# Values evicted by ScalarE, the first experts' products moved behind the routing, and a weight place opened sooner, in a two-layer graph network

## The chip, the core and the metric

The kernel runs on one core of a Trainium2 chip. A time is the device time of one execution in microseconds; the kernel before is given by the median of 4 runs. The engines are called as in the profile: PE is TensorE, DVE is VectorE, ACT is ScalarE, POOL is GpSimd, and SP is the queue that issues most of the DMAs. Each engine executes its own instructions in the order in which they are written, and waits in that order.

## The reference

384 nodes with 1024 features each, fp32, pass two layers. What matters here:

```python
xn = _layernorm(x)
x = x + _L0_gnn_ref(xn, edges, types, ...) + _L0_mix_ref(xn, ...)
x = x + _L0_ffn_ref(_layernorm(x), ...)
xn = _layernorm(x)
x = x + _L1_gnn_ref(xn, ...) + _L1_mix_ref(xn, ...)
x = x + _L1_ffn_ref(_layernorm(x), ...)

# L0_gnn: attention over the graph's edges, 16 heads
q = x @ wq.T + bq; k = x @ wk.T + bk; v = x @ wv.T + bv
q2 = q @ wiq.T + biq; k2 = k @ wik.T + bik; v2 = v @ wiv.T + biv
mask = -inf; mask[src, dst] = softplus(type_weight)[edge_type - 1]   # the last edge of a cell counts
attn = softmax(q2 @ k2.T / 8 + mask); out = attn @ v2
return out @ wo.T + bo

# L0_mix: q = softplus(q / scale), k likewise; linear attention, here over sequences of one node
# L0_ffn: logits of 8 experts from x @ wqkv.T (a small attention of 8 by 8 for each node), top 2 of 8,
#         y = (silu(a) * g) @ w2[e].T with a, g = split(x @ w1[e].T), weighted by softmax of the two
# L1_ffn: one of 8 experts by the nearest centroid of x,
#         y = x + relu((xhat * gamma[e] + beta[e]) @ w1[e] + b1[e]) @ w2[e] + b2[e], mixed with x by a sigmoid
```

A row of `attn` sums to 1, so a bias on `v2` comes out of the attention as the same bias on `out`.

## The kernel before, in words

Nodes lie in three blocks of 128 (`nb`), features in eight pieces of 128 (`KC`), and halves of 512 (`hf`). A projection is written either with its result transposed, features on the partitions (`proj_t`, the matmul at L136, `w` fixed and 384 nodes as the moving side), or with nodes on the partitions (`proj_n`, L148, 512 features as the moving side). A scheduler writes each engine's order from the program's order and its estimates, so a line of the code that is moved can land in another place on each engine.

The stages, with their time in the profiled execution:

- 0 to 15 us: the norm of the input, and its transposes into `xnT` (L203, L217, L218).
- 15.6 to 222 us: the projections q, k, then q2, k2 and v. Meanwhile POOL builds the edge mask: the edges' keys are written out and read back in every order (`keys`), DVE compares them to find repeated cells, and POOL writes 96 columns of types into a table of cells in memory, one indirect DMA after the other (`lastd`, L469); each waits for an earlier one of its table. The cells are blanked before by SP's DMAs. The table is read back into `last`.
- 222 to 265 us: `v2` (L148 for `wiv`). Its six PSUM blocks are evicted by DVE with a broadcast bias row (L551). The router's column sums `sums` (L556), eight matmuls with a matrix of ones, and their copy `wsum` (L557) come last. `kind` (L568) and the following lines to L586 turn `last` into the additive `mask` on DVE.
- 277 to 469 us: a loop over eight pairs of heads. For a pair, `scores` (L614) for each block writes one PSUM place `sc` (there is one), DVE scales and masks it into `s` (L616) and takes the row maximum `rs` (L619), ACT takes exps (L621), DVE the normalisation `rr`, `pr` (L624, L627). Between them stand the blocks of the mix heads (`mix_block`, L655), whose softplus takes ACT's pieces z, az and a few more and DVE's L229 to L232, and `values` for the pair before, whose result is copied to `oT`. `inv` and `binv` (L599 to L603) are small constants of the mix heads.
- 469 to 582 us: the output projections (L703) and the first routing, block by block. `to_router(nb)` transposes x, multiplies with the router `wr` (L746) and norms the block; `to_places(nb)` does the top 2 on DVE (L354 to L378, `both` L755), and then `place_both`: `rank` on PE (L385), `own` on DVE (L388), and the gather of the first two experts' nodes by a product with `own`, `first` (L758, 8 matmuls a block that are each recorded twice). `first` collects over the three blocks and is copied to `xe` (L770, L771). POOL scatters the normed rows to `xg0` for the other experts.
- 583 to 714 us: the experts of layer 0 (L896, L923).
- 725 to 930 us: layer 1's graph part and mix heads. Its start waits for a gather `yt` of the experts' results.
- 930 to 994 us: the projection `w_fc` (L1105) and the second routing, built like the first: `mix_norm` (L1116, L1117), transposes, `x` times centroids `cen` (L1138), norms, `near` (L1160), `place` (`rank` L328, `slotf` L337), `own` (L1169), `first` (L1172), and its eviction with the experts' gamma and beta (`scaled`, L961 to L968).
- 996 to 1079 us: the experts of layer 1 (`h` L1311, `t` L1320, `y` L1335, L1337), the rows of the others read by SP (`xs`, L1300).

Weights are loaded by SP in one order into a ring of places (`ring`, `next_w`), each load waiting until its place has been read. There are three places from the start, one (`w_top`) more from the attention, two more (`w_more`) from the first routing, and one (`w_last`) that `experts1_sorted` opens.

The places differ in when they open: a pool's memory can be taken when the pools that lay there before have been closed and read.

## Time and profile before

| | |
|---|---|
| median of 4 runs | 1081.91 us (1077.88 to 1086.05) |
| the profiled execution | 1087.65 us, its span 1085.8 us |
| mean granted clock of PE | 0.973 |
| PE busy | 1022.4 us, 94% of the span |
| DVE, ACT, POOL busy | 349.0, 267.1, 317.5 us |
| memory traffic | 172 GB/s over the span; 399 GB/s in the second of 40 slices (27 to 54 us) |

A busy share is over the whole span. A row of the timeline gives start, duration, engine, line, operation, result and sources, the shapes, and in brackets the engine's idle time just before and what ended it. A row with x16 is a run of 16 records of one kind; an fp32 matmul leaves two records. `PEclk` and the durations of records of one shape tell which clock PE had: a run of 16 records of 128x128 by 128 spans about 2 us at full clock and 3.8 at half.

### The profile page before, as it was taken

How to read it: one execution, taken by the hardware profiler on the slowest of the kernel's cores; microseconds unless marked ns; L12 is line 12 of the kernel's file. 1: busy time of each engine (PE TensorE's matmuls, PEld its weight loads, DVE VectorE, ACT ScalarE, POOL GpSimd, SP SyncE). 2: the span in 40 equal slices, each digit the busy share in tenths (PEclk: the TensorE clock that was granted, in tenths of full speed). 3: DMA queues.
4: the chain of work that ended last, by engine and by line, in shares of the span. 5: the costliest groups of instructions: out<-in, count | busy, mean ns of one | idle time of the engine just before them, and what ended most of it. 6: DMA issues, size and time to landing. Idle time of an engine off the chain costs nothing. (4 is left out here: it accounts for less than half of the span.)

```text
span 1085.8 us, 9492 instructions
## 1 busy us (share of the span) xinstructions
PE 1022.4 (94%) x3453; PEld 552.4 (51%) x3453; DVE 349.0 (32%) x966; ACT 267.1 (25%) x493; POOL 317.5 (29%) x276
## 2 busy tenths in 40 slices
PE   6999999997799999999997999969999999997896
PEld 4555555543455555544555666434444466555332
DVE  4580000006676667621332111051306000554121
ACT  3111111100576666620112111221302010122211
POOL 2152355564787668600001000130002000014100
PEclk9999999999899999999997999979999999998998
DMA  9949623226223432523165988968522222136992
GB/s 340 399 157 408 161 88 146 79 80 186 11 0 41 117 78 0 156 78 126 58 199 208 318 311 289 380 230 324 193 78 78 78 78 83 72 117 245 360 410 111
DMA packets 69973, 186.53 MB, mean 172 GB/s; under 512 B 21416, under 2 KB 22280, under 8 KB 69664
## 3 DMA queue, kind: packets, MB, share of 16 engines
q1 hardware_dynamic: 41216, 150.19, 38.4%
q0 software_dynamic: 24688, 29.40, 11.1%
q10 hardware_dynamic: 4016, 6.27, 1.6%
q8 instruction: 29, 0.48, 0.2%
q14 instruction: 24, 0.20, 0.1%
HBM read 161.29 MB, written 25.06 MB: 172 GB/s over the span
## 5 line engine op out<-in xcount | busy, mean ns | idle before, releaser
L469 POOL DMA_INDIRECT countd<-seen,cells x96 | 153.2, 1596 | 62.6 <-DMA countd<-seen,cells 38.2
L136 PE MATMUL mm<-xnT,w 128*128 128x384 f32 x512 | 165.7, 486 | 0.3 <-DVE xnT L218 0.3
L655 PE MATMUL mm<-xnT,w 128*128 128x384 f32 x384 | 133.4, 495 | 0.0
L136 PEld LDWEIGHTS mm<-xnT,w 128*128 128x128 f32 x512 | 97.1, 190 | 67.9 <-DVE xnT L218 0.6
L469 POOL DMA_INDIRECT lastd<-typ,cells x96 | 96.2, 1002 | 118.7 <-DMA lastd<-typ,cells 75.2
L655 PEld LDWEIGHTS mm<-xnT,w 128*128 128x128 f32 x384 | 71.0, 191 | 57.4 <-issue 14.9
L703 PE MATMUL mm<-w,t 128*128 128x512 f32 x192 | 84.5, 594 | 0.8 <-DVE x L402 0.8
L148 PE MATMUL mm<-w,xnT 128*128 128x512 f32 x192 | 82.8, 592 | 0.0
L136 PE MATMUL mm<-t,w 128*128 128x384 f32 x256 | 82.7, 486 | 0.0
L896 PE MATMUL h<-w,xeT 128*128 128x352 f32 x224 | 68.3, 462 | 0.7 <-DVE xeT L888 0.3
L136 PEld LDWEIGHTS mm<-t,w 128*128 128x128 f32 x256 | 48.6, 190 | 33.9
L148 PEld LDWEIGHTS mm<-w,xnT 128*128 128x128 f32 x192 | 36.3, 190 | 45.5 <-issue 45.5
L568 DVE TENSOR_TENSOR kind<-last 128x1152 f32<-128x1152 f32 x1 | 1.4, 1358 | 177.1 <-DMA last<-lastd 177.1
L703 PEld LDWEIGHTS mm<-w,t 128*128 128x128 f32 x192 | 35.8, 190 | 43.6 <-issue 41.7
L896 PEld LDWEIGHTS h<-w,xeT 128*128 128x128 f32 x224 | 41.9, 190 | 24.4 <-DVE xeT L888 2.4
L1005 PE MATMUL mm<-w,xnT 128*128 128x512 f32 x96 | 43.6, 613 | 1.3 <-DVE xnT L218 1.3
L292 POOL DMA_INDIRECT xg<-xn,slot x3 | 4.0, 1323 | 139.4 <-DVE xn L1116 122.6
L1105 PE MATMUL mm<-w,oT 128*128 128x512 f32 x96 | 42.7, 595 | 0.0
L923 PE MATMUL y<-w,hT 128*128 128x512 f32 (+1 forms) x96 | 41.6, 592 | 0.0
L148 PE MATMUL mm<-w,t 128*128 128x512 f32 x96 | 41.4, 592 | 0.0
L516 ACT ACTIVATE t<-mm,cols 128x384 f32<-128x384 f32 x24 | 13.9, 580 | 107.3 <-PE mm L136 98.1
L1060 POOL TENSOR_TENSOR x<-x,gb 128x1024 f32<-128x1024 f32 x3 | 7.3, 2427 | 98.4 <-DVE x L1059 98.4
(297 smaller groups left out, 1188.3 us busy)
## 6 DMA issues: line engine op xcount, KB each, us to landing
w<-in_w1s SPq DMA_DIRECT2D x16, 1408.0 KB, 7.7
w<-in_xw SPq DMA_DIRECT2D x8, 2048.0 KB, 15.9
w<-in_xw2s SPq DMA_DIRECT2D x8, 2048.0 KB, 14.9
w<-in_w2s SPq DMA_DIRECT2D x8, 1536.0 KB, 10.8
keys<-keyd POOLq DMA_DIRECT2D x4, 1536.0 KB
xg<-blank SPq DMA_DIRECT2D x12, 512.0 KB, 11.5
w<-in_wk SPq DMA_DIRECT2D x2, 2048.0 KB
w<-in_mwq SPq DMA_DIRECT2D x2, 2048.0 KB, 7.8
```

Source lines behind the costliest of these rows:

```text
L136: mm(ps[:, :N], lhsT=w[:, j, kc, :], rhs=rhs[:, kc, :], start=kc == 0, stop=kc == KC - 1)
L148: mm(ps, lhsT=lhs[:, kc, nb * P:(nb + 1) * P], rhs=w[:, kc, :], start=i == 0 and kc == 0, stop=i == len(pairs) - 1 and kc == KC - 1)
L292: i = gp.indirect_dma_start(rows, bass.IndirectOffsetOnAxis(ap=at, axis=0), src, None, bounds_check=n - 1, oob_is_err=False)
L469: gp.indirect_dma_start(cells[:, :], bass.IndirectOffsetOnAxis(ap=at[:, i, c:c + 1], axis=0), src[:, c:c + 1], None, bounds_check=N * N + ...
L516: ac.activation(dst[:, ob, :], ps, AF.Identity, bias=cols[:, i, ob:ob + 1], scale=1.0)
L655: mm(ps[:, :N], lhsT=w[:, j, kc, :], rhs=xnT[:, kc, :], start=kc == 0, stop=kc == KC - 1)
L703: mm(pss[hf], lhsT=src[:, kc, nb * P:(nb + 1) * P], rhs=w_out[("mwo", "wo")[part]][hf][:, kc, :], start=part == 0 and kc == 0, stop=part = ...
L896: mm(ag[i][:, :F0], lhsT=xeT[kc // 4][:, kc % 4, :], rhs=w1[kc // 4][:, kc % 4, i * F0:(i + 1) * F0], start=kc == 0, stop=kc == KC - 1)
L923: mm(y, lhsT=hT[:k, e, j, :], rhs=w2[:k, e % 2 * len(K2) + j, :], start=j == 0, stop=j == len(K2) - 1)
L1005: mm(ps, lhsT=xnT[:, kc, nb * P:(nb + 1) * P], rhs=ws[hf][:, kc, :], start=kc == 0, stop=kc == KC - 1)
L1060: gp.tensor_tensor(x[:, b, :], x[:, b, :], gb[:, 1, :], OP.add)
L1105: mm(ps, lhsT=oT[:, kc, nb * P:(nb + 1) * P], rhs=ws[hf][:, kc, :], start=kc == 0, stop=kc == KC - 1)
```

## The change

- The values' six blocks are copied out of PSUM by ACT, without the bias; the bias `biv` is added later, by feature, when `oT` leaves PSUM (a tenth column of `cols`). The broadcast rows `brow` shrink from three to two.
- The router weight `wr` is loaded first on ACT's queue, and the column sums and `wsum` are made at the start. `inv` and `binv` are made behind the second block's norm.
- The small inputs of the last stage (`b1x`, `gbx`, `cen`) are loaded by SP behind `brow`, where they were loaded by ACT's queue.
- In both routings the products `first` of blocks 0 and 1 are issued behind the last block's router, and that of block 2 behind its places. `own` is kept for all blocks. The centroids' sums `csum`, which stood at the start of layer 1, stand in the first routing behind the products of blocks 0 and 1.
- In layer 1 the buffers `ed_w`, `z`, `y`, `em` and `kv` lie in a pool `mid` that is closed ahead of the `w_fc` projections; `w_last` is opened there, and is the next place in the ring.

```diff
...
+    b1x = const.tile([P, FC1], F32, name="b1x")
+    gbx = const.tile([P, 2, X, KC], F32, name="gbx")
+    cen = const.tile([P, KC, X], F32, name="cen")
+    csum = const.tile([P, X], F32, name="csum")
     rest = ExitStack()
     with ExitStack() as layer:
         act = layer.enter_context(tc.tile_pool(name="act0", bufs=1))
...
         with tc.tile_pool(name="edges", bufs=1) as ed, tc.tile_pool(name="hot", bufs=2) as hot, \
                 tc.tile_pool(name="work0", bufs=2) as work, \
                 tc.tile_pool(name="ps_a", bufs=8, space=PSUM) as pa:
+            ac.dma_start(wr, d["wqkv"])
             ids = ed.tile([P, 3, EC], I32, name="ids")
             ac.dma_start(ids, d["ids"])
...
             wq = [load_t(d["wq"][hf], apart=hf == 0) for hf in range(2)]
...
-            cols = const.tile([P, 9, KC], F32, name="cols")
+            cols = const.tile([P, 10, KC], F32, name="cols")
             ac.dma_start(cols, d["cols"])
+            ps = pa.tile([P, HB], F32, tag="mm", name="sums")
+            for kc in range(KC):
+                mm(ps[:, :3 * X], lhsT=ones_q, rhs=wr[:, kc, :], start=kc == 0, stop=kc == KC - 1)
             ready(AF.Sqrt, eps)
             for nb in range(NB):
                 mean, rinv = norm_block(x[:, nb, :])
                 xn = work.tile([P, D], F32, tag="xn", name="xn")
                 norm_on_both(xn, x[:, nb, :], mean, rinv)
                 copied = to_t(pa, xnT, xn, nb)
+            with tc.issue_after(copied[0].ins):
+                ve.tensor_copy(wsum, ps[:, :3 * X])
             alike = ed.tile([P, P], F32, name="alike")
...
             proj_t(pa, "wq", xnT, biased(qT, 0), wq)
             kT = hidden()
             proj_t(pa, "wk", xnT, biased(kT, 1))
-            brow = ed.tile([P, 3, D], F32, name="brow")
+            brow = ed.tile([P, 2, D], F32, name="brow")
             with tc.issue_after(loads[-1].ins):
-                nc.sync.dma_start(brow, bass.AP(tensor=d["brow"].tensor, offset=d["brow"].offset, ap=[[0, P], [D, 3], [1, D]]))
-                nc.sync.dma_start(wr, d["wqkv"])
+                nc.sync.dma_start(brow, bass.AP(tensor=d["brow"].tensor, offset=d["brow"].offset, ap=[[0, P], [D, 2], [1, D]]))
+                nc.sync.dma_start(b1x, d["b1"])
+                nc.sync.dma_start(gbx[:, 0], d["xgamma"])
+                nc.sync.dma_start(gbx[:, 1], d["xbeta"])
+                nc.sync.dma_start(cen, d["cen"])
             q2T = act.tile([P, KC, N], F32, tag="q2T", name="q2T")
             proj_t(pa, "wiq", qT, biased(q2T, 3))
             with tc.issue_after(loads[-1].ins):
...
             vT = hidden()
             proj_t(pa, "wv", xnT, biased(vT, 2))
             for nb in range(NB):
-                for i in (1, 2):
+                for i in range(2):
                     ve.tensor_tensor(x[:, nb, :], x[:, nb, :], brow[:, i, :], OP.add)
             v2 = act.tile([P, NB, D], F32, tag="v2", name="v2")
             def values_in(hf, nb, ps):
                 cs = slice(hf * HB, (hf + 1) * HB)
-                ve.tensor_tensor(v2[:, nb, cs], ps, brow[:, 0, cs], OP.add)
+                ac.copy(v2[:, nb, cs], ps)
             proj_n(pa, [("wiv", vT)], values_in)
-            ps = pa.tile([P, HB], F32, tag="mm", name="sums")
-            for kc in range(KC):
-                mm(ps[:, :3 * X], lhsT=ones_q, rhs=wr[:, kc, :], start=kc == 0, stop=kc == KC - 1)
-            ve.tensor_copy(wsum, ps[:, :3 * X])
...
             with tc.issue_after(copied[1].ins):
                 ac.activation(eta, etw, AF.Abs)
             softplus(etp, etw, eta, 4)
+            inv = act.tile([P, KC], F32, name="inv")
+            with tc.issue_after(copied[1].ins):
+                ac.activation(inv, cols[:, 8, :], AF.Exp, scale=-1.0)
+            ve.tensor_scalar(inv, inv, 1.0 / 8.0, None, op0=OP.mult)
+            binv = act.tile([P, 2, KC], F32, name="binv")
+            for i in range(2):
+                ve.tensor_tensor(binv[:, i, :], cols[:, 5 + i, :], inv, OP.mult)
             kind = ed.tile([P, NB, N], F32, name="kind")
             ve.tensor_tensor(kind, lasts[0], lasts[1], OP.max)
...
-            inv = at.tile([P, KC], F32, name="inv", bufs=1)
-            ac.activation(inv, cols[:, 8, :], AF.Exp, scale=-1.0)
-            ve.tensor_scalar(inv, inv, 1.0 / 8.0, None, op0=OP.mult)
-            binv = at.tile([P, 2, KC], F32, name="binv", bufs=1)
-            for i in range(2):
-                ve.tensor_tensor(binv[:, i, :], cols[:, 5 + i, :], inv, OP.mult)
...
                         h = 2 * hp + r
                         mm(ps[r * DH:(r + 1) * DH, :N], lhsT=v2[:, mb, h * DH:(h + 1) * DH], rhs=prT[r][:, mb, :],
                            start=mb == 0, stop=mb == NB - 1)
-                ve.tensor_copy(oT[:, hp, :], ps[:, :N])
+                ve.tensor_scalar(oT[:, hp, :], ps[:, :N], cols[:, 9, hp:hp + 1], None, op0=OP.add)
             w_mix = {}
...
         def row(cols, name, dtype=F32):
             return kp.tile([P, *cols], dtype, name=name)
-        keep = {"xe0": [row([KC // 2, P], f"xe0_{g}") for g in range(2)], "oh": row([NB, X], "oh4"), "most": row([NB], "most4"),
+        keep = {"xe0": [row([KC // 2, P], f"xe0_{g}") for g in range(2)], "oh": row([NB, X], "oh4"), "own": row([NB, P], "own4"), "most": row([NB], "most4"),
                 "slot": row([NB], "slot4", I32), "info": row([NB, 2], "info4"),
                 "slots": row([NB, 2], "slots6", I32), "share": row([2, NB], "share6")}
...
                 oh = route_block(*queries[nb], share[:, 1, nb:nb + 1])
                 ve.tensor_tensor(both[:, nb, :], oh[0], oh[1], OP.add)
                 place_both(px, slots[:, nb, :], own0[:, nb, :], both, oh, nb)
+                scatter(xg0[:, :], [slots[:, nb, i:i + 1] for i in range(2)], [xn[:, nb, :]] * 2, X * CAP0)
+            def to_first(nb):
                 for kc in range(KC):
                     mm(first[kc // 4][:, kc % 4, :], lhsT=xn[:, nb, kc * P:(kc + 1) * P], rhs=own0[:, nb, :],
                        start=nb == 0 and kc % 4 == 0, stop=nb == NB - 1 and kc % 4 == 3)
-                scatter(xg0[:, :], [slots[:, nb, i:i + 1] for i in range(2)], [xn[:, nb, :]] * 2, X * CAP0)
             for nb in range(1, NB):
                 pss = halves(pm)
...
                 project(nb, 1, pss)
                 to_places(nb - 1)
             to_router(NB - 1)
+            for nb in range(NB - 1):
+                to_first(nb)
+            ps = px.tile([P, HB], F32, tag="x", name="sums")
+            for kc in range(KC):
+                mm(ps[:, :X], lhsT=ones_q, rhs=cen[:, kc, :], start=kc == 0, stop=kc == KC - 1)
             to_places(NB - 1)
+            to_first(NB - 1)
             ve.tensor_copy(keep["xe0"][0], first[0])
             ac.copy(keep["xe0"][1], first[1])
...
+            ve.tensor_copy(csum, ps[:, :X])
             over0 = too_many(px, "x", both, CAP0)
...
     K2V = P + 2
-    b1x = const.tile([P, FC1], F32, name="b1x")
-    ac.dma_start(b1x, d["b1"])
-    gbx = const.tile([P, 2, X, KC], F32, name="gbx")
-    ac.dma_start(gbx[:, 0], d["xgamma"])
-    ac.dma_start(gbx[:, 1], d["xbeta"])
-    cen = const.tile([P, KC, X], F32, name="cen")
-    ac.dma_start(cen, d["cen"])
     def scaled(dst, src, g, es):
...
+            mid = ExitStack()
+            part = mid.enter_context(tc.tile_pool(name="mid", bufs=1))
             a_bc = act.tile([P, 2, D], F32, tag="rows", name="a_bc")
-            ed_w = act.tile([P, NB, N], F32, name="ed_w")
-            if keep is not None:
-                csum = act.tile([P, X], F32, name="csum")
-                ps = px.tile([P, HB], F32, tag="x", name="sums")
-                for kc in range(KC):
-                    mm(ps[:, :X], lhsT=ones_q, rhs=cen[:, kc, :], start=kc == 0, stop=kc == KC - 1)
-                ve.tensor_copy(csum, ps[:, :X])
+            ed_w = part.tile([P, NB, N], F32, name="ed_w")
             xn1 = act.tile([P, NB, D], F32, name="xn1")
             xnT = act.tile([P, KC, N], F32, tag="byf", name="xnT2")
...
                    lambda hf, nb, ps: ac.copy(vh[:, nb, hf * 4:hf * 4 + 4, :P], ps.rearrange("p (a b) -> p a b", b=P)))
             if taken:
                 held(loads[-2:], taken)
-            kv = act.tile([P, KC, K2V], F32, name="kv")
+            kv = part.tile([P, KC, K2V], F32, name="kv")
             threes = (range(0, 3), range(3, 6), range(6, 8))
             for hps in threes:
                 n = len(hps)
...
                 to_t(pm, oT, o, nb)
             ws = [load_w(d["w_fc"][hf]) for hf in range(2)]
+            mid.close()
+            if keep is not None:
+                w_last = rest.enter_context(tc.tile_pool(name="w_last", bufs=LAST, side="right", reuse_waits="tile"))
+                ring[:0] = [w_last] * LAST
             def project(nb, hf):
                 ps = pm.tile([P, HB], F32, tag="mm", name="mm")
                 for kc in range(KC):
...
             xT = act.tile([P, KC, N], F32, tag="kq", name="xT4")
             oh, most, slot = keep["oh"], keep["most"], keep["slot"]
             first = [px.tile([P, HB], F32, tag="x", name="first").rearrange("p (a b) -> p a b", b=P) for _ in range(2)]
+            own = keep["own"]
             sums, last = {}, []
             def to_router(nb):
...
                 slotf = small.tile([P, 1], F32, tag="slotf", name="slotf")
                 place(px, "x", slotf, oh, oh, nb, CAP)
-                own = work.tile([P, HB], F32, tag="y", name="own")[:, :P]
-                ve.tensor_scalar(own, rowf[:, :P], slotf, None, op0=OP.is_equal)
+                ve.tensor_scalar(own[:, nb, :], rowf[:, :P], slotf, None, op0=OP.is_equal)
                 ve.tensor_copy(slot[:, nb:nb + 1], slotf)
-                for kc in range(KC):
-                    mm(first[kc // 4][:, kc % 4, :], lhsT=xb[:, kc * P:(kc + 1) * P], rhs=own,
-                       start=nb == 0 and kc % 4 == 0, stop=nb == NB - 1 and kc % 4 == 3)
                 with tc.issue_after(scatter(xg[:, :], [slot[:, nb:nb + 1]], [xb], X * CAP).ins):
                     gp.tensor_tensor(x[:, nb, :], x[:, nb, :], fb, OP.add)
                     last[:] = [scatter(bg[:, :], [slot[:, nb:nb + 1]], [x[:, nb, :]], X * CAP)]
+            def to_first(nb):
+                for kc in range(KC):
+                    mm(first[kc // 4][:, kc % 4, :], lhsT=xn1[:, nb, kc * P:(kc + 1) * P], rhs=own[:, nb, :],
+                       start=nb == 0 and kc % 4 == 0, stop=nb == NB - 1 and kc % 4 == 3)
             for hf in range(2):
                 project(0, hf)
...
                 project(nb, 1)
                 to_places(nb - 1)
             to_router(NB - 1)
+            for nb in range(NB - 1):
+                to_first(nb)
             to_places(NB - 1)
+            to_first(NB - 1)
             for g in range(2):
                 scaled(keep["xe0"][g], first[g], g, (0, 1))
             at = [slot[:, nb:nb + 1] for nb in range(NB)]
...
     def experts1_sorted(xe0):
-        with tc.tile_pool(name="w_last", bufs=LAST) as w_last, \
-                tc.tile_pool(name="act4", bufs=1) as act, \
+        with tc.tile_pool(name="act4", bufs=1) as act, \
...
-            ring.extend([w_last] * LAST)
```

## The prediction

> **What bounds the kernel now.** I read the busy shares first, then the list of waits of TensorE (PE), then the timeline around the long waits. PE works for 1022.4 of 1085.8 us, so the change can win only inside the 63 us in which PE stands still, inside work that it takes off PE (little), or by the clock. The longest waits of PE (columns: what waited for what, total us, times, longest):
>
> ```profile
> engine line waited for: us in total, times, longest us
> PE sc L614 <- DVE wsum L557: 11.8, 1, 11.8
> PE mm L217 <- DVE xn L203: 10.3, 1, 10.3
> PE mm L217 <- DMA yt<-yg,slots: 8.7, 1, 8.7
> PE rank L385 <- DVE both L755: 5.0, 1, 5.0
> ```
>
> The first and the last lie where the change works; the second is the start (unchanged), the third the gather between the layers. The timeline at the first (start, us, engine line operation, idle before and who ended it):
>
> ```profile
> 263.34 1.86 PE L556 MATMUL sums<-wr,ones_q 128*128 128x24 f32 x16
> ...
> 273.22 3.67 DVE L551 TENSOR_TENSOR v<-mm,brow 128x512 f32<-128x512 f32 x6
> ...
> 276.81 0.17 DVE L557 COPY wsum<-sums 128x24 f32<-128x24 f32 x1
> 276.96 1.28 ACT L599 ACT_TABLE_LOAD   x1 [54.04 <-DVE v L551]
> ...
> 277.04 1.65 PE L614 MATMUL sc<-k2T,q2T 64*128 64x384 f32 x4 [11.84 <-DVE wsum L557]
> ...
> 278.87 0.95 DVE L616 SCALAR_TENSOR_TENSOR s<-sc,mask 128x768 f32<-128x768 f32 x1
> ```
>
> The reader sees that PE has all of its operands by 265.2, and that DVE, in its own order, evicts the six value blocks only after the mask chain (254.26 to 273.22), which starts when `last` has been read back:
>
> ```profile
> L568 DVE TENSOR_TENSOR kind<-last 128x1152 f32<-128x1152 f32 x1 | 1.4, 1358 | 177.1 <-DMA last<-lastd 177.1
> ```
>
> So two things end there, the evictions and, just behind them, the mask. The timeline of the two routings:
>
> ```profile
> 572.43 0.22 DVE L364 TENSOR_REDUCE r_s<-r_qk 128x8 f32<-128x64 f32 x1 [0.32 <-ACT r_qk L361]
> ...
> 574.03 0.23 DVE L366 TENSOR_TENSOR r_qk<-r_qk,r_q 128x64 f32<-128x64 f32 x1 [1.15 <-ACT none L197]
> ...
> 578.55 3.79 PE L758 MATMUL first<-own,xn 128*128 128x128 f32 x16 [0.52 <-DVE own L388]
> ```
>
> ```profile
> 981.64 2.05 PE L1172 MATMUL first<-own,xn 128*128 128x128 f32 x16 [2.39 <-DVE slot L1170]
> ...
> 984.94 1.95 PE L1138 MATMUL x<-cen,xT 128*128 128x8 f32 x16 [0.38 <-DVE xT L218]
> ...
> 990.33 3.78 PE L1172 MATMUL first<-own,xn 128*128 128x128 f32 x16 [1.18 <-DVE slot L1170]
> ```
>
> The same 16 matmuls take 2.05 us at full clock and 3.78 at half: a wait of 5.0 or 11.8 us is followed by a slow stretch (267.0 to 280.7 and 574.2 to 587.9 by the record lengths), one of 2.65 us ahead of 981.64 is not.
>
> **Part 1, values by ACT.** ACT idles 54.04 us before 276.96, and its eviction of 128x512 takes 0.58 us (row L771), so v2 is there as PE delivers, and the first `sc` runs near 264: the sums (1.86 us) have left this place too. That does not give back 11.84 + 1.86, since the next step waits for the mask. PE does sc(0,0) and the q block (265 to 270.4); sc(0,1) shares its PSUM place with sc(0,0), which DVE frees only with s(0,0), now straight behind the mask at 273.25 instead of 278.87. The chain from there, by rows: s 0.95, rs 0.95, then the exps. ACT's table load for them (1.28 us), hidden before behind the `inv` that stood at 276.96, is now queued behind ACT's wait for rs and is exposed. Exps 1.4, rr and pr 1.0, s(0,1) 0.95, then ACT's softplus pieces of the q block (z 0.67, az 0.52, a part 0.52, two table loads, Ln 0.61) to 282.8, exp(0,1), rr, pr, s(0,2) to 286.0, and sc(1,0) at about 286.05. Before it ran at 293.52, and from there PE never waits within the loop. Gain: **-7.5**. Bounds: sc(0,1) alone comes 10.7 sooner (274.25 for 284.99), which counts if PE and not this chain sets the rest; if one more 3.41 us stretch of half clock follows the new waits of 3 to 4 us, 1.7 is lost, giving -5.8. I take the chain.
> The Trainium skill (ScalarE: Activation LUTs, "What ACT_TABLE_LOAD costs") gives about 1.28 us for the load and about 1.38 more for a drain before it, 2.66 in all for a switch; the trace shows 1.28, and ACT has nothing to drain here. By the larger figure this term would be -6.1.
>
> The eviction of oT with a per-feature bias (tensor_scalar, 0.54 by the row of that shape) replaces a copy of about the same time: 0, covered by DVE's 68% idle; uncovered it would be 8 x 0.1.
>
> **Part 2, the start and the loads.** The 96 KB of wr go to ACT's queue ahead of ids, which is issued some 0.45 us later; the 8 sums matmuls now open PE's queue and wait for wr, which should land by 8, before the first transposes at 10.27. POOL's key and scatter chain, behind ids, may start 0.1 to 0.6 later. Against it SP's broadcast brow falls from 1.5 to 1.0 MB (b1x, gbx, cen add 0.11, wr's 0.1 leaves) ahead of the `keys` read; at 400 GB/s (page, second slice) 0.5 MB is 1.3 us. The chain of 96 scatters, then `last`, then the mask move with it one for one: **-1.0**, from +1 (only the delay) to -3 (each of the DMA waits in the slow stretch shortened as well). ACT's waiting DMA issues there leave for SP, which is idle.
>
> **Part 3, routing 0.** first(0) (1.78 net of overlap) leaves the place between projections, first(1) (1.45 of it) the middle of block 2's router: -3.2. All 16 matmuls come back in block 2's routing, five between the transposes and 11 behind the router with 8 sums matmuls, where PE waits 5.0 us anyway: 11 x 0.224 + 8 x 0.23 = 4.3, hidden if DVE's chain does not wait. But the copy `csum` stands in DVE's order between L360 and L364, and waits for these sums: L366 comes some 5.0 us after the router's end instead of 3.05, +1.95. Behind it on DVE stands all the rest of the routing, and PE's rank behind that. Net **-1.3**; bounds -3.2 (csum's wait covered) and +0.7 (both gone and the matmuls partly cold: 1.95 - 1.3).
> The sums at L984 (1.95 us) lie in the 8.7 us gather wait: 0, and no more than -1.95.
>
> **Part 4, routing 1.** first(0) leaves (-1.78), and PE then has nothing between 977.2 and 981.1, for first(1) no longer fills the wait for x(2): a gap of 3.9 us. The router of block 2 comes at about 983.75 (984.94 before), but 15 of the 16 moved matmuls (3.36 us) stand in PE's order ahead of rank(2), behind which place, own and slot wait: own at 991.6 instead of 990.19, **+1.4** at full clock. The clock decides the rest. If the gap costs one half-rate stretch, 1.7 more; if first(2) then runs at full clock, -1.8, and its successor h (8.78, warm 7.09) another -1.7. Ends: 1.4 - 1.9 - 1.7 = -2.2 and 1.4 + 3.2 (all 15 cold) = +4.6. 3.9 us is a little nearer the 5.0 that lost the clock than the 2.65 that kept it: I take one lost stretch and half of first(2)'s gain, 1.4 + 1.7 - 0.9 = **+2.2**.
>
> **Part 5, the weight place.** SP may load one expert weight some 26 us earlier. No PE wait on a DMA stands in 996 to 1079 (its waits there are for DVE and ACT): 0. SP's order now puts it ahead of the gather xs1 (issued 994.68); if that lands late, the 3.6 us of h waits for xeT grow by as much, at most one load of 2048 KB, 5 us at 400 GB/s.
>
> **Sum.** -7.5 - 1.0 - 1.3 + 2.2 = -7.6. The profiled execution took 1087.65 us (span 1085.8, 1.85 around it), 5.74 above the median of the runs shown; 1080.05 for such an execution, 1074.3 against the median. 0.5%, 5.4 us, is about what a measurement of this kernel tells from no change.
>
> **Rivals.**
> A. Layer 1 eats it: the clock falls in the 3.9 us gap and the 15 matmuls run cold (+4.6), routing 0 at +0.7. -7.5 - 1.0 + 0.7 + 4.6 = -3.2, 1078.7. For it: 5.0 us lost the clock. Against: 2.65 did not, and the matmuls fill the next stretch.
> The Trainium skill (TensorE: Matmul & The Clock Gate, "Why this matters for your kernels") asks for no PE gaps above about 3 us between bursts; by that, 3.9 loses the clock. The trace agrees at 5.0 and 2.65 and has nothing between.
> B. More: the scatter chain gains its 3 us and the clock holds: -7.5 - 3 - 1.3 - 2.2 = -14, 1067.9. For it: the scatters wait 75.2 us for DMAs. Against: the cells' blanking, which slows them, is not smaller.
> C. Slower: the scatter chain slips. In 127 to 180 us POOL issues 33 instructions in 53 us, in 78 to 127, while the cells are blanked (324 GB/s), 14 in 49: 1.6 against 3.5 us each. Each scatter more that falls into the crowded stretch costs 1.9 us at the mask, one for one. From 7 of them (13 us) the kernel is slower by over 0.5%; at 8, 15.2 - 7.6 = +7.6, 1089.5. For it: the blanks are issued behind a weight load which the changed loads could move. Against: SP's traffic ahead of it shrinks.
>
> **How the numbers follow.** Forecast 0.52 (its own range -11 to -4, 0.06 of it within 0.5%), A 0.21, B 0.13, C 0.14. Faster 0.46 + 0.13 = 0.59, within 0.06 + 0.21 = 0.27, slower 0.14. From B's end, 1067.5, to above A, 1083, the range leaves out C and some of B.
>
> **What would show it.** First `sc` near 264 with no wait for wsum, and sc(1,0) some 7 us sooner; `kind` at about 253; a DVE wait of `csum` for the sums in routing 0; rank(2) of layer 1 behind the firsts and own 1.4 us later relative to the router's old place; no new DMA wait of PE behind 996. Wrong if `kind` moves by more than 3 us, or if the attention loop waits for ACT beyond sc(1,0).

## The result, and the profile after

The changed kernel takes 1075.08 us (median of 42 runs, 1073.73 to 1081.92), the kernel before 1081.17 us (68 runs, 1076.64 to 1090.66). The ratio is 0.9946, 95% interval 0.9933 to 0.9959: 5.8 us, or 0.54%, faster. The forecast was 1074.3. Measured again later on one chip, 12 runs of the changed kernel against 35 of the kernel before, the ratio was 0.9998 (0.9966 to 1.0030); how both can be so is the last point of the explanation. The profiled executions are 1085.8 and 1077.2 us long, 8.6 apart, which is more than the medians differ.

In what follows sc(p,b) is the score of pair p and block b, both counted from 0; rank(b) and first(b) are the small `rank` matmul and the products `first` of block b. A trace is one profiled execution. The clock granted to PE is recorded in each trace as stretches at 1 and at 0.5, called full and half clock here.

The waits of PE after the change (what waited for what, total us, times, longest):

```profile
engine line waited for: us in total, times, longest us
PE mm L217 <- ACT xn L204: 12.0, 1, 12.0
PE sums L440 <- DVE bmv L173: 7.8, 1, 7.8
...
PE mm L217 <- DVE x L1129: 3.8, 1, 3.8
...
PE rank L385 <- DVE both L766: 2.5, 1, 2.5
...
PE sc L624 <- ACT v L565: 0.7, 1, 0.7
```

The 11.8 us ahead of the attention are 0.7 now, the 5.0 of the first routing 2.5. New are 3.8 us in the second routing, 7.8 at the start (where PE waited 10.3 before), and the wait between the layers has grown from 8.7 to 12.0. The timeline of the changed kernel around the attention's start:

```profile
265.20 0.59 ACT L565 COPY v<-mm 128x512 f32<-128x512 f32 x1 [6.28 <-PE mm L148]
265.83 0.92 PE L624 MATMUL sc<-k2T,q2T 64*128 64x384 f32 x4 [0.68 <-ACT v L565]
266.68 5.43 PE L666 MATMUL mm<-xnT,w 128*128 128x384 f32 x16
267.85 0.96 DVE L626 SCALAR_TENSOR_TENSOR s<-sc,mask 128x768 f32<-128x768 f32 x1 [0.19 <-DVE mask L604]
...
269.86 1.28 ACT L631 ACT_TABLE_LOAD   x1 [4.08 <-DVE rs L629]
...
272.04 0.92 PE L624 MATMUL sc<-k2T,q2T 64*128 64x384 f32 x4
...
280.91 0.92 PE L624 MATMUL sc<-k2T,q2T 64*128 64x384 f32 x4 [0.26 <-DVE s L626]
```

The values leave PSUM as PE delivers, `s` of the first score starts as soon as the mask is there, the table load stands exposed behind `rs`, and sc(1,0) runs at 280.91 where it ran at 293.52. sc(0,1), at 272.04, follows the 16 matmuls of L666 without a wait: its PSUM place was free at 268.81, when `s` ended. The two routings, PE and DVE:

```profile
559.18 0.17 DVE L795 COPY csum<-sums 128x8 f32<-128x8 f32 x1 [3.12 <-PE sums L786]
...
562.55 0.57 PE L385 MATMUL rank<-both,later 128*128 128x8 f32 x2 [2.52 <-DVE both L766]
```

```profile
968.48 1.84 PE L217 MATMUL mm<-ident,x 128*128 128x128 f32 x8 [3.84 <-DVE x L1129]
970.94 1.88 PE L1151 MATMUL x<-cen,xT 128*128 128x8 f32 x8 [0.61 <-DVE xT L218]
972.67 0.77 PE L1189 MATMUL first<-own,xn 128*128 128x128 f32 x2
973.23 1.71 PE L1151 MATMUL x<-cen,xT 128*128 128x8 f32 x8
974.80 5.61 PE L1189 MATMUL first<-own,xn 128*128 128x128 f32 x30
...
982.55 3.62 PE L1189 MATMUL first<-own,xn 128*128 128x128 f32 x16 [0.90 <-DVE own L1181]
```

DVE waits 3.1 us for sums that it does not need there. In the second routing PE has half clock from 968.8, just behind the gap of 3.84 us, to 979.0 (transposes 1.84 us against 1.04 before, the router's 16 records 3.6 against 1.95), and again from 982.5 to 985.9, under the 16 records of first(2); rank(2) stands behind the products of blocks 0 and 1.

To compare kernels, the execution is cut at five matmuls of PE, read off the timelines: the first projection, the first score of the second pair of heads (sc 1,0), the first `h` of layer 0's experts, the first router product of layer 1, the first `h` of the last stage, and the end of the last matmul. "Mask" is the start of `kind`. All in us; the last five columns are the lengths of stretches.

| profiled execution | mask starts | first projection | to sc(1,0), from 0 | to layer 0's `h` | to layer 1's router | to the last stage's `h` | to the end |
|---|---|---|---|---|---|---|---|
| before | 254.26 | 15.63 | 293.52 | 289.49 | 369.42 | 44.24 | 81.69 |
| before, another trace | 244.50 | 15.19 | 285.08 | 291.12 | 368.93 | 44.22 | 81.69 |
| changed | 248.43 | 17.29 | 280.91 | 287.61 | 370.99 | 49.23 | 81.02 |
| changed, another trace | 242.56 | 17.00 | 280.40 | 287.64 | 370.86 | 49.21 | 81.02 |

### The profile page after: what moved, and what is told of

It reads as the page before. It is cut to its first block, busy times and chain, and to the rows that moved or that the text cites. A ratio compares the mean times of both kernels' runs of the same rounds, so it can differ in the third digit from the quotient of the medians.

```text
span 1077.2 us, 9493 instructions
## 1 busy us (share of the span) xinstructions
PE 1025.8 (95%) x3453; PEld 556.8 (52%) x3453; DVE 344.7 (32%) x960; ACT 270.7 (25%) x499; POOL 318.6 (30%) x276
## 5 line engine op out<-in xcount | busy, mean ns | idle before, releaser
L666 PE MATMUL mm<-xnT,w 128*128 128x384 f32 x384 | 132.4, 493 | 0.0
L666 PEld LDWEIGHTS mm<-xnT,w 128*128 128x128 f32 x384 | 70.5, 190 | 56.4 <-issue 13.4
```

Source lines behind the costliest of these rows:

```text
L666: mm(ps[:, :N], lhsT=w[:, j, kc, :], rhs=xnT[:, kc, :], start=kc == 0, stop=kc == KC - 1)
```

## The experiments

The theory after the result: the attention gives most; routing 0 gives 2; the second routing takes 5, by the clock and by the order of PE; and the size of the first depends on when the edge mask is ready, which differs between executions of one kernel. Rivals: the loads or the start made the gain; the second routing's loss is the clock of one execution.

**The kernel before, a second trace (before_look).** No edit.

> The kernel before, looked at once more. Its runs lie in two groups, about 1077 to 1080 and 1084 to 1090; the profiled one was of the later group. Theory A (collision): what divides them is whether the two reads of `last` (2 x 576 KB) meet the 2 MB load of the mix weight. In a run near 1078 the mask chain starts at 251 or sooner, in a run near 1087 at about 254 as before. Rival (the clock or a later stage divides them): the mask chain starts at 254 in a run near 1078 too, and the difference is found behind 300 us.

Measured: 1080.22 us. The start of the mask in this trace (groups of instructions: line, engine, shapes | busy, mean | idle before, who ended it), to be held against the 177.1 us of idle DVE in the execution that the forecast used, and the first score from its timeline:

```profile
L568 DVE TENSOR_TENSOR kind<-last 128x1152 f32<-128x1152 f32 x1 | 1.4, 1358 | 168.4 <-DMA last<-lastd 168.4
...
267.66 1.65 PE L614 MATMUL sc<-k2T,q2T 64*128 64x384 f32 x4 [2.91 <-DVE wsum L557]
```

The mask starts at 244.50, 9.8 us sooner, and PE waits 2.9 us for the first `sc`, not 11.8. So the wait that the forecast was built on was that of one late execution. Two things came late there: the last of the 96 scatters went out at 242.1 instead of 236.1, and the second read of `last`, issued at 245.0 behind the 2 MB load of wk (issued 242.93), took 9.3 us to the mask's start instead of 6.0.

**The load of wk held back (before_hold; after_hold is a second trace of the same kernel).**

```diff
                 w_mix[wname] = load_t(d[wname][ob // 4])
+                if wname == "mwk" and ob == 0:
+                    held(loads[-1:], read)
```

> The kernel before, with the one change that the load of the first mix weight (wk, 2 MB) waits until the second read of `last` has landed. Theory A (collision): the read takes 5.7 us from its issue as after the change, not 9.3; the mask chain starts some 3.6 us sooner than 254.26, and the median falls by up to 0.4%, with fewer runs in the later group. Rival: the scatter chain itself sets the start of the mask, and the median stays within 0.1%.

> The same kernel as the run before, a second look at its front: under theory A the mask chain again starts within 6 us of the issue of the second read of `last`; under the rival its start varies by 3 us or more between the two looks.

Measured: 1079.63 us, ratio 1.0002 (0.9979 to 1.0024). The reads took 5.4 and 6.0 us to the mask's start (245.15 and 245.35), as the theory said, but the median did not move, so the rival holds for the median. The later traces bear the theory out for single executions: in sums_gap and first1_late, where the load was issued with the second read or 0.3 us behind it, the mask came 8.2 and 10.1 us after the read's issue; in every trace where the load came 1.8 us or more behind the read, 5.1 to 6.0.

**Part 1 alone (values_only).** The kernel before with ACT's copies, the bias at `oT` and two broadcast rows:

```diff
-                ve.tensor_tensor(v2[:, nb, cs], ps, brow[:, 0, cs], OP.add)
+                ac.copy(v2[:, nb, cs], ps)
...
-                ve.tensor_copy(oT[:, hp, :], ps[:, :N])
+                ve.tensor_scalar(oT[:, hp, :], ps[:, :N], cols[:, 9, hp:hp + 1], None, op0=OP.add)
```

> The kernel before with part 1 alone: ACT evicts the values, the bias by feature is added when oT leaves PSUM, the broadcast rows are two. The forecast's theory: sc(0,0) at 265.2, s(0,0) right behind the mask; with the mask at 273.2 sc(1,0) at about 286 instead of 293.5, -7.5, and with a mask as early as 267.7 the loop is bound by PE and sc(1,0) comes at 280.3 (265.2 + 15.1). Everything behind moves with it: ratio about 0.993. Rival: this part is worth little by itself and the gain of the change comes from the loads and the start: ratio above 0.998.

Measured: 1121.94 us, ratio 1.0393 (1.0356 to 1.0431), slower by 4%, which neither theory had. The waits and the timeline of this kernel show where:

```profile
engine line waited for: us in total, times, longest us
PE mm L136 <- ACT k2T L516: 44.9, 1, 44.9
```

```profile
260.22 1.28 ACT L599 ACT_TABLE_LOAD   x1 [83.52 <-DVE mask L586]
261.51 0.21 ACT L599 ACTIVATE inv<-cols 128x8 f32<-128x8 f32 x1
261.63 0.56 ACT L516 ACTIVATE k2T<-mm,cols 128x384 f32<-128x384 f32 x1
...
262.24 8.28 PE L136 MATMUL mm<-xnT,w 128*128 128x384 f32 x16 [44.88 <-ACT k2T L516]
```

`inv` (L599) waits for the mask: it lies in a pool that is opened behind the edges' and, as this wait suggests, takes over memory of theirs. In this kernel it stands ahead of the evictions of k2T on ACT's queue, and ACT stands for 83.5 us with PE behind it. The change makes `inv` early and in another pool, a line of the diff that the prediction costed as a table load. The next run puts this to the test.

**Part 1 with `inv` and `binv` as the change has them (values_inv).**

```diff
+            inv = act.tile([P, KC], F32, name="inv")
+            with tc.issue_after(copied[1].ins):
+                ac.activation(inv, cols[:, 8, :], AF.Exp, scale=-1.0)
...
-            inv = at.tile([P, KC], F32, name="inv", bufs=1)
-            ac.activation(inv, cols[:, 8, :], AF.Exp, scale=-1.0)
```

> The kernel before with part 1 as the change has it: values by ACT, the bias later, two broadcast rows, and `inv` and `binv` made behind the second block's norm. Theory: without `inv` in the way, the first `sc` comes at about 265.4 (behind the sums) without a wait for the mask, PE is bound from there while the mask starts before 247 or so, and sc(1,0) lies at about 280.5 instead of 285: 4 to 5 us less than the kernel before where its mask starts at 244.5 to 245.4, ratio 0.995 to 0.997. Everything from the first routing on as in the kernel before (44.2 and 81.7). Rival: the evictions by ACT delay exps or weights elsewhere, ratio above 0.999.

Measured: 1074.33 us, ratio 0.9959 (0.9940 to 0.9978). The wait of ACT is gone. Mask at 241.47, sc(1,0) at 280.64; later stretches 289.47, 369.37, 44.25 and 81.68, as before the change.

```profile
265.79 0.92 PE L614 MATMUL sc<-k2T,q2T 64*128 64x384 f32 x4 [0.37 <-DVE wsum L557]
```

So part 1 alone, with the smaller broadcast, is worth 0.41%, 4.4 us. On the same chip the whole change has 0.9998 (next run): what it adds to part 1 costs about 4 us there.

**The changed kernel again, and its second routing (after_look, first1_back, fill1, sums_gap: one chip, the same 35 runs of the kernel before).**

> The changed kernel again, beside the next three on the same chip. Three looks at the kernel before (one with a load held back, which changed nothing in the median) started the mask chain at 244.5 to 245.4, not 254.3, and took 44.2 us from the first router product of layer 1 to its first `h`, and 81.7 from there to the end. Expected: 49.2 and 81.0 again, since no clock phase explains the first and the weight place the second; first `sc` behind the values without a wait above 1 us; median 1074 to 1076. Rival: both numbers belong to one execution's clock phase, and lie elsewhere here.

Measured: 1078.48 us (1074.50 to 1086.15), ratio 0.9998 (0.9966 to 1.0030). The stretches are 49.21 and 81.02 again (table).

first1_back puts the products back behind each block's places:

```diff
                 ve.tensor_copy(slot[:, nb:nb + 1], slotf)
+                to_first(nb)
...
             to_router(NB - 1)
-            for nb in range(NB - 1):
-                to_first(nb)
             to_places(NB - 1)
-            to_first(NB - 1)
```

> The changed kernel with the products `first` of the second routing back behind each block's places. Theory: the stretch from layer 1's first router product to its first `h` falls from 49.2 to about 44.2 as before the change, and the median by 4 to 5 us, to about 1070.5. Rival (the products only fill PE's time, wherever they stand): within 1 us of the changed kernel.

Measured: 1072.52 us, ratio 0.9950 (0.9925 to 0.9975), 6.0 below the changed kernel beside it; the stretch is 45.82. Its timeline of PE:

```profile
970.27 3.68 PE L1190 MATMUL first<-own,xn 128*128 128x128 f32 x16 [2.39 <-DVE slot L1182]
973.77 1.06 PE L217 MATMUL mm<-ident,x 128*128 128x128 f32 x8
975.18 1.95 PE L1151 MATMUL x<-cen,xT 128*128 128x8 f32 x16 [0.35 <-DVE xT L218]
...
980.67 3.64 PE L1190 MATMUL first<-own,xn 128*128 128x128 f32 x16 [1.18 <-DVE slot L1182]
```

In this trace the clock fell at 970.4, behind the wait of 2.39 us (3.68 us for the 16 records), where it held behind the same wait in the kernel before (2.05); that makes the 1.6 us over 44.2. It was back at 973.8, for the transposes.

fill1 leaves the order and fills the gap with eight matmuls whose result nothing reads:

```diff
+            ps = px.tile([P, HB], F32, tag="x", name="filler")
+            for kc in range(KC):
+                mm(ps[:, :P], lhsT=ones_q, rhs=ones_q, start=kc == 0, stop=kc == KC - 1)
             to_router(NB - 1)
```

> The changed kernel with eight matmuls on constants (their result is not read) put into the gap of 3.8 us ahead of the last block's transposes in the second routing; the products stay behind the router. If the clock that is lost in this gap makes the loss: transposes 1.04 us, router about 2, the 16 products 3.6 instead of 6.4, and the stretch falls from 49.2 to about 45, median -4. If the order makes it (rank behind 15 products, 3.4 us at full clock): the stretch stays above 47.5, median -1.5 at most.

Measured: 1077.76 us, ratio 0.9973 (0.9950 to 0.9997), 0.7 below the changed kernel by the medians and 2.7 by the ratios, whose ranges overlap; the stretch is 48.90.

```profile
964.53 2.03 PE L1201 MATMUL filler<-ones_q 128*128 128x128 f32 x16
968.51 1.84 PE L217 MATMUL mm<-ident,x 128*128 128x128 f32 x8 [1.95 <-DVE x L1129]
970.36 3.58 PE L1151 MATMUL x<-cen,xT 128*128 128x8 f32 x16
973.80 6.40 PE L1189 MATMUL first<-own,xn 128*128 128x128 f32 x32
```

The filler ran at full clock and halved the gap, and the clock fell all the same: half from 969.0 to 979.2 and from 982.6 to 986.1, as in the changed kernel. So the run does not tell clock from order, as it was meant to; it tells that this filling with short matmuls did not hold the clock.

sums_gap puts the centroids' sums back into the wait for the gather:

```diff
             ed_w = part.tile([P, NB, N], F32, name="ed_w")
+            if keep is not None:
+                ps = px.tile([P, HB], F32, tag="x", name="sums")
+                for kc in range(KC):
+                    mm(ps[:, :X], lhsT=ones_q, rhs=cen[:, kc, :], start=kc == 0, stop=kc == KC - 1)
+                ve.tensor_copy(csum, ps[:, :X])
```

> The changed kernel with the centroids' sums and their copy back at the start of layer 1, in the wait for the gather. Theory: in the first routing L366 comes 3.0 us behind the router's end instead of 4.7, which gives 1.5 to 1.9, and the graph part of layer 1 runs with less of its first matmuls at half clock, as the sums keep PE busy in a wait of 12 us, which gives up to 1.3: median 1.5 to 3.2 lower. Rival: DVE's wait for the sums is hidden, the clock falls either way: within 0.7 us.

Measured: 1074.78 us, ratio 0.9968 (0.9943 to 0.9993), 3.7 below the changed kernel, where 1.5 to 3.2 was expected. From layer 0's `h` to layer 1's router it needs 367.54 instead of 370.9, but this cannot all be put down to the sums: 2.1 us of it is the first `h` of layer 0, which ran at full clock here (9.73 us for its 32 records, 11.87 and 11.80 in the changed kernel), as it did in first1_late, where the sums had not been put back. In the first routing the time from the last block's rank sums (550.66 in the changed kernel, 557.15 here) to the last products (564.06, 569.57) falls from 13.40 to 12.42. This trace had a late mask (252.18) and shows what that costs after the change: PE waited 4.4 us for `s` (3.2 the longest).

**The order alone (first1_late).** All products behind the last block's places:

```diff
             to_router(NB - 1)
-            for nb in range(NB - 1):
-                to_first(nb)
             to_places(NB - 1)
-            to_first(NB - 1)
+            for nb in range(NB):
+                to_first(nb)
```

> The changed kernel with all products of the second routing behind the last block's places in the program: on PE, rank(2) then stands behind 5 matmuls of the products and not behind 15, and 19 of them follow while DVE makes `own`. Theory (the order makes half of the loss, the clock the other): the clock is still lost in the 3.8 us ahead of the transposes, but `own` comes 2 to 4 us sooner, the stretch from the first router product to `h` is 45.5 to 47.5 instead of 49.2, median -2 to -3.5 against the changed kernel. Rival (the clock alone): as the changed kernel within 0.7.

Measured: 1074.83 us, ratio 0.9969 (0.9951 to 0.9988; the changed kernel on the same chip 0.9998). The stretch is 46.84. PE's timeline of this kernel:

```profile
970.22 1.97 PE L217 MATMUL mm<-ident,x 128*128 128x128 f32 x8 [3.84 <-DVE x L1129]
...
976.96 2.48 PE L1189 MATMUL first<-own,xn 128*128 128x128 f32 x10
979.24 0.43 PE L328 MATMUL rank<-oh,later 128*128 128x8 f32 x2
979.52 6.03 PE L1189 MATMUL first<-own,xn 128*128 128x128 f32 x38
```

The gap is the same and the clock falls in the same place, for 13.7 us in one piece (969.1 to 982.8); the changed kernel has 13.7 us ahead of its `h` too, in two pieces. rank(2) stands behind five products, and PE works through the rest while DVE makes `own`. With as much half clock in both, 2.4 of the 5.0 us are put down to the order. Behind the stretch the first `h` of the last stage ran at full clock (7.09 us instead of 8.78). It did so in last_back too, which has the changed kernel's order, so that this comes from the order is not shown.

The same trace has a mask that starts at 254.23, within 0.03 us of the execution that the forecast used:

```profile
274.58 0.92 PE L624 MATMUL sc<-k2T,q2T 64*128 64x384 f32 x4 [2.64 <-DVE s L626]
...
286.30 0.92 PE L624 MATMUL sc<-k2T,q2T 64*128 64x384 f32 x4 [1.42 <-DVE s L626]
```

These are sc(0,1) and sc(1,0), forecast for 274.25 and 286.05.

**The weight place back (last_back).** `w_last` opened by the last stage:

```diff
             mid.close()
-            if keep is not None:
-                w_last = rest.enter_context(tc.tile_pool(name="w_last", bufs=LAST, side="right", reuse_waits="tile"))
-                ring[:0] = [w_last] * LAST
```

> The changed kernel with the weight place opened where it was before, by the last stage. Theory: the stretch from the first `h` of the last stage to the last matmul is 81.7 us in each look at the kernel before and 81.0 in two of the changed kernel; if the weight place makes this, it is 81.7 here, and the median is up by 0.7 or nothing that can be told. Rival (the clock, or the order of the `y`): 81.0 again.

Measured: 1079.35 us, ratio 1.0003 (0.9982 to 1.0023), against 0.9998 of the changed kernel: no difference that can be told. The trace has another clock in both stretches (47.90 and 83.00; half clock for 10.2 us ahead of `h` and not under it), so they cannot be compared as they are. The six traces of the kernel before and of variants with its last stage have 81.67 to 81.69 to the end, the four with the place opened sooner and the same clock 81.02. Where the difference lies can be read in the last expert's `y`, here and in the changed kernel:

```profile
1059.15 4.51 PE L1349 MATMUL y<-w,hT 128*64 128x512 f32 x18 [0.23 <-DVE hT L1342]
1060.24 3.84 PE L1350 MATMUL y<-w,hT 128*64 128x512 f32 x16 [0.23 <-DVE hT L1343]
```

All seven traces with the place opened by the last stage have 18 records in 4.50 or 4.51 us and then 14 in 3.65; all seven with it opened sooner have 16 in 3.84 and 16 in 3.65. So 0.66 us go with the place, as another order of the same 32 records on PE, and not as a wait for a load; the times cannot tell it.

**A better version (best).** first1_back and sums_gap together, and on ACT's queue the router weight ahead of the input's second block:

```diff
-    for nb in range(NB):
-        (nc.scalar if nb % 2 else nc.sync).dma_start(x[:, nb, :], d["x"][nb * P:(nb + 1) * P, :])
+    for nb in (0, 2):
+        nc.sync.dma_start(x[:, nb, :], d["x"][nb * P:(nb + 1) * P, :])
...
             ac.dma_start(wr, d["wqkv"])
+            ac.dma_start(x[:, 1, :], d["x"][P:2 * P, :])
```

> The changed kernel with three mends: the second routing's products back behind each block's places, the centroids' sums back in the gather wait of layer 1, and the router weight issued first on ACT's queue, ahead of the input's second block. Theory: the stretch from layer 1's first router product to `h` falls from 49.2 to 44.2 to 46; L366 of the first routing comes 3 us behind the router and not 4.7; the sums of the start run some 1 us sooner than 7.8 and PE's first projection starts at 16 or before, not at 17.0 to 17.3. Median 1068 to 1071, ratio to the kernel before 0.990 to 0.994. Rival: the three places overlap (a late mask takes back what the start gives), and it is not below the run with the products back alone (1072.5, ratio 0.995).

Measured: 1070.40 us (1066.82 to 1076.07), ratio 0.9927 (0.9897 to 0.9957); the profiled span is 1065.5. On another chip first1_back had 0.9950 (0.9925 to 0.9975): the ranges overlap, so that the other two mends add to it is not shown by times. Stretches: first projection at 16.28, sc(1,0) at 279.56, then 286.04, 367.18, 44.20 and 81.02. The start in this kernel:

```profile
5.14 3.58 PE L441 MATMUL sums<-wr,ones_q 128*128 128x24 f32 x16 [5.14 <-DMA wr<-in_wqkv]
11.29 4.64 PE L217 MATMUL mm<-ident,xn 128*128 128x128 f32 x24 [2.57 <-DVE off L202]
16.28 3.17 PE L136 MATMUL mm<-xnT,w 128*128 128x384 f32 x9 [0.35 <-DVE xnT L218]
```

## Why the prediction was right or wrong

The time came out inside the range, 0.8 us from the forecast, and the sign was right. The nearness is luck in part: the terms were wrong in opposite directions, and the largest was priced on an execution with a late mask. Between the two profiled executions:

| step | forecast | measured |
|---|---|---|
| attention and mask (parts 1 and 2) | -7.5 - 1.0 = -8.5 | 280.91 - 293.52 = -12.6 |
| routing 0 (part 3) | -1.3 | 287.61 - 289.49 = -1.9 |
| sums taken from the gather's wait (part 3) | 0 | 370.99 - 369.42 = +1.6 |
| routing 1 (part 4) | +2.2 | 49.23 - 44.24 = +5.0 |
| weight place (part 5) | 0 | 81.02 - 81.69 = -0.7 |
| sum | -7.6 | -8.6 |

**Part 1.** For the mask that it took, the forecast was right in mechanism and size: first1_late, with the mask at 254.23, has sc(0,1) and sc(1,0) waiting for `s` and sc(1,0) at 286.30, 7.2 us ahead of 293.52 where 7.5 was forecast. In the profiled execution of the changed kernel another thing binds. The mask came at 248.43, the first `s` and the exposed table load of 1.28 us stand where the forecast put them, but sc(0,1) waits for PE's own work and not for `s`; PE waits 0.7 and 0.3 us in all up to there, and PE, not the chain over DVE and ACT, sets sc(1,0). That is the forecast's other bound ("which counts if PE and not this chain sets the rest"). The base was one execution as well: the other trace of the same kernel has the mask at 244.50, where `sc` waits 2.9 us and not 11.8, and part 1 (values_inv) is worth 4.4 us over many executions, not 7.5. The mask moves the end one for one only while it ends last. The line with 177.1 us of idle DVE named the release, but said nothing on how much it varies; the 24 waits on scatters of 75.2 us in all would have been a reason to ask.

**Part 2.** The -1.0 for fewer bytes cannot be seen: the mask starts between 242.6 and 254.2 in the eight traces with the changed front and at 244.5 and 254.3 in the kernel before. The two traces with the smaller broadcast and the old loads have 240.5 and 241.5, the soonest of all, but two traces of a thing that varies by ten us show no gain. That it differs from execution to execution was rival C's matter, with the sign open; it came as the scatter chain and, in three traces, as a read beside a weight load. The start was wrong: wr landed by 8 as forecast (the sums start at 7.83), but their time was put at nothing. They took 3.58 us, where the same 16 records took 1.86 at L556, and PE was not free until 11.2, 1.0 later than the transposes began before. The first projection starts at 16.7 to 17.3 in seven traces instead of 15.2 to 16.3. In the best version the sums start at 5.14 and are done in time, but the transposes still begin at 11.29, now waiting for the norm, and the projection starts at 16.28: 0.4 to 1.0 us come back, in one trace.

**Part 3.** The wait of `csum` was there (3.12 us on DVE), and -1.3 against -1.9 is within the bounds. Taking it away gave 1.0 between rank and products (13.40 to 12.42), not the 1.95 of the forecast: L366 comes 4.7 us behind the router's end with the wait, and still 3.7 in the best version without it, where it waits for ACT. The sums "in the 8.7 us gather wait" were put at "0, and no more than -1.95", and +1.6 was measured. Most of this lies in the first 32 matmuls behind the wait, here in values_inv (sums in the wait), the changed kernel and first1_late:

```profile
714.99 15.65 PE L1005 MATMUL mm<-w,xnT 128*128 128x512 f32 x32 [0.54 <-DVE xnT L218]
713.76 16.90 PE L1012 MATMUL mm<-w,xnT 128*128 128x512 f32 x32 [0.53 <-DVE xnT L218]
716.95 15.47 PE L1012 MATMUL mm<-w,xnT 128*128 128x512 f32 x32 [0.53 <-DVE xnT L218]
```

With the sums in the wait they take 15.4 to 15.7 us in eight traces. With the sums gone, PE idles 11.9 to 12.0 us in one piece, and they take 16.8 to 17.1 in five traces out of six. The sixth is first1_late, with the same wait and 15.47. So the loss goes with the missing sums mostly, and the clock can hold without them; what decides is not shown.

**Part 4.** Rival A's mechanism, not the forecast's, and a little beyond its bound (+4.6). The forecast took one lost stretch of 3.4 us and half of first(2)'s gain; the trace has half clock for 13.7 us ahead of `h`, first(2) included, where the kernel before has 6.8 (987.3 to 994.1). first1_late gives 2.4 us to the order, where the forecast had +1.4 at full clock; the rest, 2.6, goes to the clock by subtraction alone. The clock's part also varies with the order unchanged: the second piece of half clock, 3.4 us under first(2), came in both traces of the changed kernel and in fill1 (49.2, 49.2, 48.9), and stayed away in sums_gap and last_back (47.4, 47.9), behind the same wait of 0.9 us. Putting the products back gave 44.20 in the best version.
The prediction read the wait ahead of 981.64 as 2.65 us; its row has 2.39.
The Trainium skill (TensorE: Matmul & The Clock Gate, "Why this matters for your kernels") asks for no gap above about 3 us. The gap of 3.84 lost the clock in each of the five traces that have it, as it says. But a wait of 2.39 lost it in first1_back and kept it in the kernel before and in the best version, 1.95 behind a filler lost it in fill1, and in the kernel before it fell at 987.3, with no wait above 0.4 us since 981.64: by these rows the length of the last wait alone does not decide.

**Part 5.** Costed at 0, since no wait for a load stood there. None came; the 0.7 us are another order of the last expert's `y` on PE, by the rows, and the times do not tell it.

**The two ratios.** The changed kernel's runs gather at about 1074.5 with a granted clock of 0.981 and about 1078.5 with 0.977; both traces, with the 49.2 us, are of the second group. By estimate, 0.004 of 1077 us are 4.3 us of clock. The 42 runs were mostly of the first group. Of the 12 in the later measurement three lie near 1074.7, five near 1078.6, and three from 1084 to 1086; a late mask would put them there, but none of these was profiled. No execution of the first group was profiled, so that it keeps its clock in the second routing is argued; that this can happen is seen in sums_gap and last_back. The kernel before differs too: 27 of its 68 runs in the first measurement are above 1083 us, but only 15 of the 98 in the four later ones, and their medians are 1077.4 to 1078.5 instead of 1081.17. The one trace of such a run (1087.65) had the late mask, which the change makes cheaper; that the others had it is argued. So the change's worth is not one number: it depends on how often the mask is late in the kernel before, and on the clock after.

## What to carry to other kernels

A wait read in one profiled execution is one draw: where a chain of many small DMAs releases it, look at a second execution before pricing what removes it. Work moved out of a wait can cost more than it saves: in five traces of six the work behind the emptied wait ran 1.1 to 1.7 us longer. Products moved behind a router should not stand ahead of the small matmul on whose result the next engine waits. When a part is tried alone, take its neighbours along that only seem to be tidying: `inv`, left where it was, made a gain of 4 us a loss of 43.

## What the runs showed of the hardware

- The chain of 96 scatters issued its last between 236.1 and 242.1 us in four traces of the front of the kernel before, with the same bytes each time.
- In the second routing with the products behind the router the clock fell to half between 967.6 and 969.6, for 10.2 us in five traces and for 13.7 in first1_late. In all six it came back while PE worked through products of 128x128 by 128. In sums_gap and last_back it then held behind a wait of 0.9 us, and first(2) took 2.05 us; in the changed kernel and fill1 it fell again behind the same wait, and first(2) took 3.5 to 3.6.
- Two reads of 576 KB took 8.2 to 10.1 us from the second's issue to their use in the three traces where a load of 2 MB was issued between 2.1 us ahead of the second read and 0.3 us behind it, and 5.1 to 6.0 where the load came 1.8 us behind or later.
